# Flamingo-style gated block on one core: seven block products for eight at two more places, and one batch's layer-norm statistics on ScalarE

## The chip, the cores and the metric

The kernel runs on one core of a Trainium2 chip. The metric is device time in microseconds, the median of three runs. Names of the engines: PE is TensorE (matmul; PEld is its weight load), DVE VectorE, ACT ScalarE, POOL GpSimd, SP SyncE (which here only issues DMAs).

## The reference

```python
def fake_quant(x, scale, zp):              # scale 8/255, zp 128
    q = jnp.clip(jnp.round(x / s + z), 0.0, 255.0)
    return (q - z) * s
def xattn(x1, x2):                         # (2,1024,2048) by (2,2048,2048)
    return jnp.matmul(fake_quant(x1, ...), fake_quant(x2, ...))
def ffn(x, weight):                        # weight (2048,2048)
    s = 127.0 / jnp.clip(jnp.max(jnp.abs(x), axis=-1, keepdims=True), 1e-05, None)
    xq = jnp.clip(jnp.round(x * s), -128.0, 127.0) / s
    scale_w = 1.0 / jnp.clip(jnp.mean(jnp.abs(weight)), EPS, None)
    tw = jnp.clip(jnp.round(weight * scale_w), -1.0, 1.0)
    return jnp.einsum('bsi,oi->bso', xq, tw) / scale_w
...
x = x + jnp.tanh(g_xattn[0]) * xattn(_layernorm(x), ctx_4096)
x = x + jnp.tanh(g_ffn[0]) * ffn(_layernorm(x), weight)
```

x is (2, 1024, 2048), the context (2, 2048, 2048), one matrix for each batch; the ternary weights serve both batches.

## The kernel before, in words

**Tiles.** The 2 x 1024 rows are 16 tiles of 128, t = 0 to 7 for batch 1 and 8 to 15 for batch 2. A product of a row tile has 2048 columns, in halves h of 1024 and quarters q of 512. `resid` has eight rows of slots, so the x of tile t + 8 is loaded where tile t stood, once that one's output has been stored.

**First product.** `norm1` (L536) takes a pair of tiles: mean and variance on DVE (`bn_stats` L542, four to a tile; `bn_aggr` L547), a square root on ACT (L551), small DVE steps, and the quantised rows in int8 on ACT (L578). `turn_steps` (transposes on PE, L505, and casts to fp16 on ACT or DVE, L513) or `turn_far` (a transposing DMA, L478, and casts, L484) makes the transposed tile aT. `context` (L593) loads a 1 MB chunk of context, quantises it on ACT (L604) and clips it on DVE (L608). `first(t, h)` (L621) is 32 matmuls of 128 x 512 (L633) into one PSUM tile of two banks (`mm`, three of them), and one 1024-wide eviction into `resid` on DVE (L639), which also sums the row into a column of `acc`.

**Second product.** `norm2` takes the mean from `acc` (L665), squares on ACT (L671), the row maximum on DVE (L677) and quantises (L727). `qT` is the transposed result. Weights come as 1 MB rows (`weight_load`), are summed (L1001, L1003), scaled, cast (L1039), transposed on PE (L1046) and clipped to fp8 by ACT or DVE (L1054, L1056). Batch 1's tiles 0 to 3 go two by two through `couple` (L778, matmuls L770), which puts a quarter of two row tiles into the two halves of one `mm` tile and evicts each half (L754, 512 wide); tiles 4 to 7 through `plain` (L803, matmuls L816). Batch 2 goes through `seven` (L892, matmuls L941): two row tiles by two column halves by two halves of the contraction are eight block products, and by the scheme of Strassen and Winograd seven are enough, with sums of row blocks made on DVE (L906 to L913) and differences of weight blocks, T1 to T4. `differences` (L835) makes those on DVE (L853) and stores them to DRAM (L872); `bring_back` (L876) loads them when the SBUF is free; its "T3" is loaded over weights that are no longer used.

**Order.** Nothing is emitted at once. Every piece is a `step` of a planner (`Order`) with an engine (or a choice of DVE and ACT), a cost in us, a due time, what it reads and writes, and slots to take from a pool: "ar" (32 slots of the arena in SBUF), "q8" (five int8 rows), "mm" (three PSUM tiles), "tr" (two banks for transposes). The planner makes a list schedule, improves it over a list of random seeds (`shake`), and `give_out` emits every instruction in the planned order. On the chip each engine runs its queue strictly in that order; the waits between engines are put in by the framework from the data that instructions share.

There is a second path, `general`, for other zero points; it does not run.

## Time and profile before

| | |
|---|---|
| median of 3 runs | 475.76 us (475.75 to 476.7) |
| the profiled execution | 475.75 us, of which the span from first to last instruction is 473.9 us |
| granted TensorE clock | 0.999 |
| PE's first product starts | 18.47 us |
| the last of PE's waits over 0.4 us ends | 37.21 us |
| DMA | 105.33 MB, mean 222 GB/s |

The shares of busy time in 40 slices of the span, in tenths (9 is 90% or more):

```profile
PE   0499999999999999999999999999999999999994
DVE  4878977697896896669998985174673887743442
ACT  3986897786999998950356783001472745600000
PEclk9999999999999999999999999999999999999999
DMA  8999999993359758759999652039220125422133
```

PE is full from the second slice to the last but one. A slice is 11.8 us. DVE has full slices around 210 to 250 us, where the weight differences and the statistics of batch 2 lie, and few after; ACT is full from about 118 to 190 us, where the weights are quantised and transposed, and stands idle for much of 190 to 235 us and of the time after 300 us.

### The profile page before, as it was taken

To read this page: it belongs to the slowest core of one execution; us is meant where nothing else is said; L and a number is where in the kernel's file an instruction comes from. 1 tells how busy PE (TensorE), PEld (TensorE's weight loads), DVE (VectorE), ACT (ScalarE), POOL (GpSimd) and SP (SyncE) were. 2 spreads that over 40 slices of the span, in tenths; PEclk is the share of its full clock that TensorE was granted. 3 is DMA by queue.
4 is the path that set the end of the run, shared out by engine and by line. 5 is a ranking of instruction groups with operands and counts; after the bars stand their busy time and mean duration, and the time that the engine had idled before them with its cause. 6 is when DMAs were issued, how large, how long until landed. Compare 5 with 4: busy or idle time off the path is not lost.

```text
span 473.9 us, 6127 instructions
## 1 busy us (share of the span) xinstructions
PE 449.3 (95%) x2468; PEld 219.6 (46%) x2468; DVE 335.0 (71%) x528; ACT 263.9 (56%) x204; POOL 21.4 (5%) x39
## 2 busy tenths in 40 slices
PE   0499999999999999999999999999999999999994
PEld 0244444445577645444444444444444444444442
DVE  4878977697896896669998985174673887743442
ACT  3986897786999998950356783001472745600000
POOL 0000000000011111111111000000000000000000
PEclk9999999999999999999999999999999999999999
DMA  8999999993359758759999652039220125422133
GB/s 314 405 413 414 413 416 346 344 428 142 147 210 345 275 169 308 261 194 339 418 422 367 232 76 58 0 109 342 84 44 1 21 68 134 133 91 89 46 155 116
DMA packets 34528, 105.33 MB, mean 222 GB/s; under 512 B 14652, under 2 KB 14652, under 8 KB 29372
## 3 DMA queue, kind: packets, MB, share of 16 engines
q1 hardware_dynamic: 27680, 70.26, 40.1%
q0 software_dynamic: 6800, 34.61, 20.5%
q8 instruction: 21, 0.34, 0.3%
q14 instruction: 15, 0.12, 0.1%
q10 hardware_dynamic: 12, 0.00, 0.0%
HBM read 80.74 MB, written 20.97 MB: 215 GB/s over the span
## 4 chain that ended last, share of the span: by engine, by line
PE 82%; DMA 5%; DVE 5%; ACT 4%; issue 1%; SPq 0%; ACTq 0%
PE mm L633 41%; PE mm L941 20%; PE mm L816 11%; PE mm L770 8%; DMA resid<-in_x_dram 3%; DMA arena<-in_ctx_dram 2%; ACT bytes L1039 2%; PE tr L505 1%; DVE arena L1056 1%; DVE strip L677 1%; DVE arena L513 1%; PE tr L1046 1%; ACT arena L513 1%; DVE resid L754 1%; ACT arena L1054 1%
## 5 line engine op out<-in xcount | busy, mean ns | idle before, releaser
L633 PE MATMUL mm<-arena 128*128 128x512 f16 x1024 | 226.3, 380 | 3.9 <-DVE arena L608 3.9
L633 PEld LDWEIGHTS <-arena 128*128 128x128 f16 x1024 | 99.6, 98 | 120.9 <-issue 5.9
L941 PE MATMUL mm<-arena 128*128 128x512 fp8e4 x448 | 97.0, 379 | 0.0
L604 ACT ACTIVATE arena<-arena,scal 128x2048 int16<-128x2048 f32 x32 | 62.9, 1998 | 60.4 <-DMA arena<-in_ctx_dram 60.3
L754 DVE SCALAR_TENSOR_TENSOR resid<-mm,am,resid 128x1024 f32<-128x1024 f32 (+1 forms) x53 | 57.5, 1099 | 49.2 <-PE mm L941 36.2
L941 PEld LDWEIGHTS <-arena 128*128 128x128 f16 x448 | 43.9, 98 | 52.8
L639 DVE SCALAR_TENSOR_TENSOR resid<-mm,scal,resid 128x1024 f32<-128x1024 f32 x32 | 40.8, 1280 | 38.4 <-PE mm L633 36.4
L770 PE MATMUL mm<-arena 128*128 128x128 fp8e4 (+1 forms) x448 | 58.5, 288 | 0.1
L816 PE MATMUL mm<-arena 128*128 128x512 fp8e4 x256 | 56.4, 379 | 0.0
L671 ACT ACTIVATE arena<-resid,strip 128x2048 f32<-128x2048 f32 x16 | 32.0, 1998 | 27.3 <-DVE strip L665 14.2
L770 PEld LDWEIGHTS <-arena 128*128 128x128 f16 x448 | 33.5, 98 | 23.0 <-issue 0.3
L677 DVE TENSOR_REDUCE strip<-arena 128x1 f32<-128x2048 f32 x16 | 36.4, 2280 | 8.5 <-ACT arena L671 8.5
L542 DVE BATCH_NORM_STATS2 stats<-resid 128x6 f32<-128x512 f32 x64 | 40.0, 679 | 2.6 <-DMA resid<-in_x_dram 2.6
L853 DVE TENSOR_TENSOR arena<-arena 128x2048 fp8e4<-128x2048 fp8e4 x16 | 36.2, 2281 | 5.2 <-PE mm L633 5.2
L816 PEld LDWEIGHTS <-arena 128*128 128x128 f16 x256 | 24.8, 98 | 28.8
L727 ACT ACTIVATE bytes<-resid,strip 128x2048 int8<-128x2048 f32 x16 | 32.9, 2090 | 8.3 <-DVE strip L700 8.0
L578 ACT ACTIVATE bytes<-resid,strip 128x2048 int8<-128x2048 f32 (+1 forms) x17 | 33.0, 1985 | 5.9 <-DVE strip L561 5.9
L1039 ACT ACTIVATE bytes<-arena,scal 128x2048 int8<-128x2048 f32 x16 | 31.6, 2002 | 1.2 <-DVE scal L1025 1.2
L1056 DVE TENSOR_SCALAR arena<-tr 128x1024 fp8e4<-128x1024 int8 x22 | 26.2, 1217 | 4.9 <-ACT arena L1054 2.8
L513 ACT CAST arena<-tr 128x1024 f16<-128x1024 int8 x23 | 22.4, 1010 | 8.9 <-PE tr L505 8.6
L484 ACT CAST arena<-arena 128x1024 f16<-128x1024 int8 x21 | 21.6, 1041 | 7.0 <-DVE arena L484 3.8
L513 DVE CAST arena<-tr 128x1024 f16<-128x1024 int8 x17 | 20.3, 1219 | 3.2 <-PE tr L505 2.0
(63 smaller groups left out, 195.8 us busy)
## 6 DMA issues: line engine op xcount, KB each, us to landing
arena<-in_ctx_dram SPq DMA_DIRECT2D x16, 1024.0 KB, 14.0
arena<-in_L_ffn_weight_dram SPq DMA_DIRECT2D x16, 1024.0 KB, 7.6
arena<-in_ctx_dram POOLq DMA_DIRECT2D x16, 1024.0 KB, 7.5
out_dram<-resid SPq DMA_DIRECT2D x31, 512.0 KB, 3.1
arena<-in_L_ffn_weight_dram POOLq DMA_DIRECT2D x9, 1024.0 KB, 5.3
resid<-in_x_dram POOLq DMA_DIRECT2D x8, 1024.0 KB, 8.8
resid<-in_x_dram SPq DMA_DIRECT2D x7, 1024.0 KB, 17.7
awayT<-arena SPq DMA_DIRECT2D x8, 512.0 KB, 8.0
```

What stands on the lines that cost most here:

```text
L513: (nc.scalar.copy if engine == "ACT" else nc.vector.tensor_copy)(d[:, ts(h, n)], v[:, ts(h, n)])
L542: nc.vector.bn_stats(stats6[:, t % 4, c, :], res(t)[:, ts(c, 512)])
L604: nc.scalar.activation(slot16(slots[0]).bitcast(I16), s["w"], AF.Identity, scale=rs2)
L633: nc.tensor.matmul(pm[t][:, ts(q, U)], a[:, c, j, :], o[:, j, ts(q, U)], start=(c + j == 0), stop=(c + j == C),)
L639: nc.vector.scalar_tensor_tensor(v, pm[t], g1, v, ALU.mult, ALU.add, accum_out=acc[:, i : i + 1])
L677: nc.vector.tensor_reduce(s["vm"][:, n + i : n + i + 1], s["dev", t], AX.X, ALU.max)
L754: lambda: nc.vector.scalar_tensor_tensor(v, ps(), am2[:, t : t + 1], v, ALU.mult, ALU.add),
L770: nc.tensor.matmul(ps[:, o0 * P : o1 * P], a[:, c, j, :], w[:, j, o0:o1], start=(c + j == 0), stop=(c + j == C),)
L816: nc.tensor.matmul(s["pm"][:, ts(i, U)], a[:, c, j, :], w[:, j, :], start=(c + j == 0), stop=(c + j == C),)
L853: nc.vector.tensor_tensor(slot8(s[k, n])[:, w], slot8(at(a))[:, w], slot8(at(b))[:, w], op, saturate=False)
L941: nc.tensor.matmul(s[bank][:, ts(n, U)], a[:, c, j, :], v[:, c, j], start=new and c + j == 0, stop=c + j == 4, skip_group_check=not new,)
L1039: nc.scalar.activation(s["q"], wl[ot]["w"], AF.Identity, scale=sw)
```

## The change

- **`seven_first`, `context_sums`**: in batch 2's first product, columns 1024 to 2047 of tiles 10 to 15 are computed in pairs with seven products of eight matmuls each. The context's differences T1, T2 and T4 get six arena slots, T3 overwrites columns of four context units, and waits until tiles 8 and 9 have used these.
- **PSUM**: the pool "mm" has six halves for three tiles; `first`, `couple`, `plain` and `seven` take two halves (`both`), `seven_first` takes single halves. Each of its products is evicted 512 wide; `acc` gets a third column for these tiles, and `norm2` adds it.
- **Tiles 6 and 7** of batch 1 go through `seven` too, with the weight differences from SBUF (`near`). `differences` is therefore placed ahead of batch 1's last tiles (hold 150 instead of 210), and `bring_back` loads all four differences into new slots, under other gates.
- **x statistics of batch 2** (`on_act`): per tile two ACT passes with an accumulator, sum and then sum of squares about the mean.
- **Smaller**: weights ask for certain arena slots first (`w_slot`), `turn_far` leaves two slots free for qT, and `shake` draws with its own generator and another list of seeds, so the whole order is drawn anew. `two_steps` is empty.

```diff
@@ room, pools
-        if prefer is None:
+        if prefer is None and k == 2:
+            prefer = range(0, len(pool) - 1, 2)
+        elif prefer is None:
...
-    acc = const.tile([P, 2 * MT], F32, name="acc")
+    acc = const.tile([P, 3 * MT], F32, name="acc")
+    def both(slots):
+        return mm[slots[0] // 2]
-    plan = Order({"ar": NS, "q8": NB, "mm": 3, "tr": 2})
+    plan = Order({"ar": NS, "q8": NB, "mm": 6, "tr": 2})
+    on_act = set(range(MT, 2 * MT))
+    two_steps = set()
@@ norm1
+        def sum_of(i, t):
+            if "ac" not in s:
+                s["ac"] = tiny(2 * n)
+            nc.scalar.activation(junk, res(t), AF.Identity, accum_out=s["ac"][:, i : i + 1])
+        def shift():
+            s["nm"] = tiny(n)
+            nc.vector.tensor_scalar(s["nm"], s["ac"][:, 0:n], -1.0 / K, None, ALU.mult)
+        def square_of(i, t):
+            nc.scalar.activation(
+                junk, res(t), AF.Square, bias=s["nm"][:, i : i + 1], accum_out=s["ac"][:, n + i : n + i + 1]
+            )
...
+        if tiles[0] in on_act:
+            for i, t in enumerate(tiles):
+                step("ACT", 2.25, due, lambda i=i, t=t: sum_of(i, t), rd=xk(t), wr=[key("s1", i)])
+            step("DVE", 0.2, due, shift, rd=[key("s1", i) for i in range(n)], wr=[key("nm")])
+            for i, t in enumerate(tiles):
+                step("ACT", 2.25, due, lambda i=i, t=t: square_of(i, t), rd=xk(t) + [key("nm")], wr=[key("s2", i)])
...
@@ new functions after first
+    def context_sums(b, h, due, spent):
+        unit = lambda c, n: slot16(cx[b, h, c]["a"]).rearrange("p (j n) -> p j n", j=2)[:, :, ts(n, U)]
+        makers = {}
+        all_in = [cx[b, h, c]["by"] for c in range(C)] + [turned["aT", t, "by"] for t in range(b * MT, b * MT + MT)]
+        todo = (("T1", (0, 1), (0, 0)), ("T2", (1, 1), "T1"), ("T4", (1, 0), "T2"), ("T3", (1, 1), (0, 1)))
+        ones = []
+        for k, u, v in todo:
+            for c in range(4):
+                def at(v, c):
+                    if isinstance(v, tuple):
+                        return unit(4 * v[0] + c, v[1])
+                    return tx[v].rearrange("p (c j n) -> p c j n", c=4, j=2)[:, c]
+                def go(slots=None, k=k, u=u, v=v, c=c, at=at):
+                    if slots is not None:
+                        tx[k] = arena[:, slots[0] * SLOT : slots[0] * SLOT + 2 * SLOT]
+                    o = unit(c, 1) if k == "T3" else at(k, c)
+                    nc.vector.tensor_tensor(o, at(u, c), at(v, c), ALU.subtract)
+                rd, give = [], []
+                for w in (u, v):
+                    if isinstance(w, tuple):
+                        rd.append(("ca", b, h, 4 * w[0] + c))
+                        give.append(cx[b, h, 4 * w[0] + c]["by"])
+                    else:
+                        rd.append(("tx", w, c))
+                        give.append(makers[w])
+                m = step(
+                    "DVE", 0.42, due, go, rd=rd, wr=[("tx", k, c)], give=give,
+                    take=("ar", 2, 0, pairs_d) if c == 0 and k != "T3" else None,
+                    then=[spent[c], ones[c]] if k == "T3" else [makers[k]] if c else all_in,
+                )
+                if k == "T1":
+                    ones.append(m)
+                if c == 0:
+                    makers[k] = m
+        return makers
...
+    def seven_first(ta, tb, h, due, makers):
+        s = {}
+        b = ta // MT
+        by_seven.update((ta, tb))
+        W = 4 * 2 * P
+        def half(t, i):
+            return slot16(turned["aT", t])[:, ts(i, W)]
+        def sums(i, slots=None):
+            if slots is not None:
+                v = arena[:, slots[0] * SLOT : slots[0] * SLOT + 2 * SLOT]
+                s[1], s[2], s[4] = (v[:, ts(j, W)] for j in range(3))
+            if i == 0:
+                nc.vector.tensor_add(s[1], half(tb, 0), half(tb, 1))
+            elif i == 1:
+                nc.vector.tensor_tensor(half(tb, 0), half(ta, 0), half(tb, 0), ALU.subtract)
+                s[3] = half(tb, 0)
+            elif i == 2:
+                nc.vector.tensor_tensor(s[2], s[1], half(ta, 0), ALU.subtract)
+            else:
+                nc.vector.tensor_tensor(s[4], half(ta, 1), s[2], ALU.subtract)
+        qa, qb = ([("aT", t, i) for i in range(2)] for t in (ta, tb))
+        ga, gb = turned["aT", ta, "by"], turned["aT", tb, "by"]
+        by = step("DVE", 0.7, due - 3, lambda slots: sums(0, slots), rd=qb, wr=[("R", ta, 1)], take=("ar", 2, 0, pairs_d), give=[gb], then=[makers["T4"]])
+        step("DVE", 0.7, due - 3, lambda: sums(1), rd=qa[:1], wr=qb[:1] + [("R", ta, 3)], give=[ga, gb])
+        step("DVE", 0.7, due - 3, lambda: sums(2), rd=qa[:1] + [("R", ta, 1)], wr=[("R", ta, 2)], give=[ga, by])
+        step("DVE", 0.7, due - 3, lambda: sums(3), rd=qa[1:] + [("R", ta, 2)], wr=[("R", ta, 4)], give=[ga, by])
+        products = (
+            ("P1", "A", lambda: half(ta, 0), (0, 0), qa[:1], True, (ta, 0), ga),
+            ("P2", "C", lambda: half(ta, 1), (1, 0), qa[1:], True, (ta, 0), ga),
+            ("P6", "A", lambda: s[2], "T2", [("R", ta, 2)], False, (ta, 1), by),
+            ("P5", "B", lambda: s[1], "T1", [("R", ta, 1)], True, (tb, 1), by),
+            ("P7", "A", lambda: s[3], "T3", [("R", ta, 3)], False, (tb, 1), gb),
+            ("P3", "B", lambda: s[4], (1, 1), [("R", ta, 4)], False, (ta, 1), by),
+            ("P4", "A", lambda: half(tb, 1), "T4", qb[1:], False, (tb, 0), gb),
+        )
+        takes = {}
+        seen = set()
+        for k, (name, bank, left, right, need, new, dest, left_by) in enumerate(products):
+            def mult(cs, slots=None, bank=bank, left=left, right=right, new=new):
+                if slots is not None:
+                    s[bank] = mm[slots[0] // 2][:, ts(slots[0] % 2, U)]
+                a = left().rearrange("p (c j m) -> p c j m", c=4, j=2)
+                for c in cs:
+                    if isinstance(right, tuple):
+                        v = slot16(cx[b, h, 4 * right[0] + c]["a"]).rearrange("p (j n) -> p j n", j=2)[:, :, ts(right[1], U)]
+                    elif right == "T3":
+                        v = slot16(cx[b, h, c]["a"]).rearrange("p (j n) -> p j n", j=2)[:, :, ts(1, U)]
+                    else:
+                        v = tx[right].rearrange("p (c j n) -> p c j n", c=4, j=2)[:, c]
+                    for j in range(2):
+                        nc.tensor.matmul(
+                            s[bank], a[:, c, j, :], v[:, j, :],
+                            start=new and c + j == 0, stop=c + j == 4, skip_group_check=not new,
+                        )
+            for i, cs in enumerate(((0, 1), (2, 3))):
+                if isinstance(right, tuple):
+                    b_keys = [("ca", b, h, 4 * right[0] + c) for c in cs]
+                else:
+                    b_keys = [("tx", right, c) for c in cs]
+                give = [left_by]
+                if isinstance(right, tuple):
+                    give += [cx[b, h, 4 * right[0] + c]["by"] for c in cs]
+                elif right == "T3":
+                    give += [cx[b, h, c]["by"] for c in cs]
+                else:
+                    give.append(makers[right])
+                take = i == 0 and new
+                m = step(
+                    "PE", 0.855, due + 1.75 * k, (lambda f, cs: lambda slots=None: f(cs, slots))(mult, cs),
+                    rd=need + b_keys, wr=[("wc", ta, bank)], take=("mm", 1) if take else None, give=give,
+                )
+                if take:
+                    takes[bank] = m
+            t, n = dest
+            last = dest in seen or dest == (tb, 0)
+            col = 2 * (t % MT) + 1 if n == 0 else 2 * MT + t % MT
+            def add(t=t, n=n, bank=bank, last=last, col=col):
+                v = res(t)[:, h * H + n * U : h * H + (n + 1) * U]
+                kw = dict(accum_out=acc[:, col : col + 1]) if last else {}
+                nc.vector.scalar_tensor_tensor(v, s[bank], g1, v, ALU.mult, ALU.add, **kw)
+            step(
+                "DVE", 0.8, due + 1.75 * (k + 1), add, rd=[("wc", ta, bank), ("g1",)],
+                wr=xk(t, h) + ([("acc", col)] if last else []),
+                give=[takes[bank]],
+            )
+            seen.add(dest)
@@ norm2, mean
+            if t in by_seven:
+                u = 2 * MT + t % MT
+                nc.vector.scalar_tensor_tensor(
+                    m, acc[:, a : a + 1], acc[:, a + 1 : a + 2], acc[:, u : u + 1], ALU.add, ALU.add
+                )
+                nc.vector.tensor_scalar(m, m, -1.0 / N, None, ALU.mult)
@@ bring_back
-                    wt[k, n] = wt[2 + n, 0] if k == "T3" else slots[0]
+                    wt[k, n] = slots[0]
...
-                    take=None if k == "T3" else ("ar", 1, 0, home_w), dma=1.4,
+                    take=("ar", 1, 0, home_w), dma=1.4,
@@ seven
-                    b = wt[right[0], n] if isinstance(right[0], str) else wt[right[0] + n, right[1]]
+                    if isinstance(right[0], str):
+                        b = near[0][right[0], n] if near else wt[right[0], n]
+                    else:
+                        b = wt[right[0] + n, right[1]]
@@ the order of the parts
-    for t in range(4, MT):
+    near = differences(due, "SP", 150.0)
+    for t in (4, 5):
         for h in range(2):
             plain(t, h, due)
             due += 6.9
+    seven(6, 7, due, near=near)
+    due += 24.2
     s1 = due
...
-    for h in range(2):
-        for t in range(MT, 2 * MT):
-            first(t, h, due)
-            due += 6.9
+    for t in range(MT, 2 * MT):
+        first(t, 0, due)
+        due += 6.9
+    spent = []
+    for t in (MT, MT + 1):
+        spent = first(t, 1, due)
+        due += 6.9
+    makers = context_sums(1, 1, due - 12.0, spent)
+    for t in range(MT + 2, 2 * MT, 2):
+        seven_first(t, t + 1, 1, due, makers)
+        due += 12.0
...
-    differences(s1 - 40.0, "SP", 210.0)
-    bring_back(s1 + 60.0, "SP", [("acc", 2 * i) for i in range(MT)])
+    gate = {"T2": [("acc", 11)], "T1": [("R", 14, 4)], "T3": [("R", 14, 4)], "T4": [("R", 14, 4)]}
+    bring_back(s1 + 60.0, "SP", gate)
```

## The prediction

> **What bounds the kernel now.** I read the busy line first, then TensorE's waits, then the chain that ended last.
>
> ```profile
> PE 449.3 (95%) x2468; PEld 219.6 (46%) x2468; DVE 335.0 (71%) x528; ACT 263.9 (56%) x204; POOL 21.4 (5%) x39
> PE tr L436 <- ACT row L2008: 7.5, 1, 7.5
> PE tr L505 <- ACT bytes L578: 5.0, 2, 4.4
> PE mm L633 <- DVE arena L608: 3.9, 2, 3.4
> PE tr L505 <- ACT arena L513: 1.4, 1, 1.4
> 168.31 0.67 DVE resid L754
> 169.02 3.61 PE mm L770 x16
> 267.44 101.01 PE mm L633 x468
> 373.63 94.12 PE mm L941 x436
> 467.77 0.75 DVE resid L754
> ```
>
> The reader is to see that TensorE (PE) is the bound. Its waits sum to about 18 us, nearly all of it before 37 us, while the first rows and context arrive. From 40 us on the windows of 20 us show PE busy for 19.4 to 20.0 of each. The chain of waits leaves PE from 126 to 169 us, for DVE and ACT work that ends in a stall of only 0.1 to 0.3 us; from 169 us it is matmuls and transposes alone, and ends with one 512-wide eviction and its store. A 512-wide matmul costs 101.01 / 468 = 0.216 us in the chain (94.12 / 436 = 0.216); the "mean 380 ns" of the groups is a pipelined duration and is not used. So a matmul removed saves 0.216 us, unless PE then waits.
>
> **What is removed on PE.** A pair of row tiles by half the columns took 64 matmuls in `first` and takes 7 x 8 = 56 in `seven_first`: three pairs, 24 fewer. Tiles 6 and 7 took 4 x 32 = 128 in `plain` and take 112 in `seven`: 16 fewer. 40 x 0.216 = **-8.6 us**.
>
> **What moves between the other engines.** The prices come from these rows (busy sum, then mean ns of one):
>
> ```profile
> L542 DVE BATCH_NORM_STATS2 stats<-resid 128x6 f32<-128x512 f32 x64 | 40.0, 679 | 2.6 <-DMA resid<-in_x_dram 2.6
> L547 DVE BATCH_NORM_AGGREGATE strip<-stats 128x2 f32<-128x24 f32 x16 | 3.8, 251 | 0.3
> L1003 ACT ACTIVATE junk<-arena 128x2048 int8<-128x2048 f32 x8 | 15.2, 1902 | 3.1 <-DMA arena<-in_L_ffn_weight_dram 3.0
> L1003 ACT ACTIVATION_READ_ACCUMULATOR junk<-arena 128x1 f32 x8 | 1.5, 186 | 0.0
> L671 ACT ACTIVATION_READ_ACCUMULATOR arena<-resid,strip 128x1 f32 x16 | 3.0, 190 | 0.0
> L906 DVE TENSOR_TENSOR arena<-arena 128x1024 f16<-128x1024 f16 x4 | 2.7, 686 | 0.1
> L754 DVE SCALAR_TENSOR_TENSOR resid<-mm,am,resid 128x512 f32<-128x512 f32 x18 | 13.3, 746 | 11.7 <-PE mm L770 10.8 <-PE mm L941 0.9
> 200.00:220.00 20.00, 20.00 (x95) 9.02 (x93) 16.22 (x14) 8.01 (x5) 3.19 (x5) 1.00 0.70 241
> 220.00:240.00 20.00, 20.00 (x94) 9.07 (x93) 19.93 (x22) 4.31 (x3) 3.04 (x5) 1.00 1.01 413
> 240.00:260.00 20.00, 20.00 (x106) 9.59 (x105) 17.45 (x33) 12.67 (x9) 1.81 (x3) 1.00 1.02 390
> 260.00:280.00 20.00, 20.00 (x106) 9.50 (x105) 18.75 (x40) 14.70 (x12) 0.53 (x1) 1.00 0.53 176
> 280.00:300.00 20.00, 20.00 (x94) 9.11 (x93) 9.44 (x13) 8.32 (x8) 0.00 (x0) 1.00 0.28 53
> ```
>
> The windows give, after the length, the busy us of PE, weight load, VectorE (DVE), ScalarE (ACT) and GpSimd.
>
> DVE loses 32 x 0.679 + 8 x 0.251 = 23.7 us of batch 2's statistics. It gains 16 context sums (`context_sums`) and 12 row sums of 0.686, 19.2; 4 row sums for tiles 6 and 7, 2.7; 21 evictions of 0.746 in place of 6 of 1.280 (L639), 8.0; 7 evictions of 1.281 in place of 4 (L754, 1024 wide), 3.8; and six small ones of 0.2. Net about +11, of which 19.2 + 8.0 fall after 280 us, where the windows show DVE half idle. On the path: nothing as a sum; what counts is who waits at each hand-over, below.
>
> ACT gains 8 x (1.902 + 0.186) for the sums and 8 x (1.998 + 0.190) for the squares (L671's Square is 1998 ns): 34.2 us. The rows of 200 to 300 us hold 48.0 of 100, so they would hold 82.2. ACT's queue is in program order: behind each x pass stand context quantisations (L604) and casts of transposed rows (L513), and PE waits for these. Walking the changed order with these durations, the transposed rows of tile 9 are ready about 5 us before PE reaches them, and those of 14 and 15 over 10 us before. So the cost taken is 0; if the cover fails it is the second rival.
>
> The DMA steps keep their kinds and order on SP and GpSimd up to the weight loads. The weight differences (L853) are made earlier and still stored away; tiles 6 and 7 use them from SBUF. The bring-backs are gated later, and land about 5 us before their products. `bring_back`'s "T3" takes new slots, so it no longer waits for the weights it overwrote. Cost 0.
>
> **What the change adds: waits inside the PSUM tiles.** `seven_first` counts a two-bank tile of PSUM as two halves and gives different block products to the two halves of one tile. In the changed program the waits follow whole tiles: a product into one half waits for the eviction of the other, and an eviction waits for the latest matmul into either half. The trace has this case already: `couple` puts two row tiles into the halves of one tile, and the rows at 168.31 and 169.02 show the matmuls for the second half starting 0.04 us after the first half's eviction ended, though the transposes before them were done at 168.88.
>
> The price of one such wait, if nothing stands between: the last matmul of 373.63 + 94.12 starts near 467.37 and its eviction at 467.77, 0.40 later; the eviction takes 0.75, PE follows 0.04 later, and 0.216 is the matmul's own slot: 0.40 + 0.75 + 0.04 - 0.216 = 1.0 us. The pairs (10,11), (12,13), (14,15) are interleaved, and the changed order has four of them bare: P2 of the second pair behind P5 of the first; half of P3 of the first behind P2 of the second; half of P7 of the second behind P4 of the first; half of P3 of the third behind its own P2. Three more are covered by four to eight matmuls (0.86 to 1.73 us) except for 0.1 to 0.2. 4 x 1.0 + 3 x 0.13 = **+4.4 us**. Bounds: 0 if the halves are independent on the chip; 7 x 1.0 = 7 if the covered ones are not covered.
>
> The Trainium skill, "PSUM — Partial Sum Buffer", section "Summary: rules for kernel authors", says that reading PSUM while a matmul runs is done by targeting a different bank, with semaphores by bank. The halves here are different banks, so by the page no wait would be needed, and the sum would be 4.4 us lower; the rows at 168.31 and 169.02 show that this program waits all the same, and I go by them.
>
> **The redrawn order.** The planner's random draws change, so the whole order does. In the head, the first weight clip shifts PE's first product from 18.47 to about 19.5, and tile 5's transposes stand behind a context quantisation whose data lands at 51; walked through, PE is 0.4 us further behind its work at 100 us: **+0.4**, bounds 0 and 1.5. From 100 to 200 us the order before loses 1.4 us (PE's start minus its summed work grows from 21.45 at 108 to 22.86 at 193). In the changed one two half-tile waits in `couple` are bare (0.95 and 0.45) and the rest roughly covered: 1.4 again, so **0**, bounds -1.4 and +2. The end is the same as before: four matmul pieces, a 512-wide eviction, a 256 KB store.
>
> Sum on the profiled execution: 473.9 - 8.6 + 4.4 + 0.4 = 470.1 us of span. The execution took 475.75, 1.86 more than its span, and the median is 475.76, so the forecast is **472.0 us**, 0.8% faster. About 0.2% (1 us) is what a measurement of this kernel can tell from no change.
>
> **Rivals.** *The halves cost nothing*: the evictions stay off PE's path. For it: DVE is half idle after 280 us. Against: the rows at 168.31. 472.0 - 4.4 = 467.6. 20%.
>
> *No change, by VectorE ahead of the pairs*: the planner counts 0.42 us for a context sum, L906 says 0.686; 16 x 0.266 = 4.3 us of lateness just ahead of `seven_first`, with its row sums and evictions queued behind. P5's row sum is ready only about 1 us early, so 3.3 could reach PE: 475.3. Against: DVE's idle share there can absorb it. 9%.
>
> *Slower, by ScalarE at the batch boundary*: ACT was idle 52.0 of 200 to 300 us, but 26.2 of that ended with context landing (15.5, 4.7, 2.9, 2.8, 0.2 of its L604 groups), which the x passes can't freely fill if they stand behind a late load; DMA is at 1.01 and 1.02 in two windows. Then 25.8 is left for 34.2, ACT ends 8.4 late, and PE waits for tile 9's or a later tile's rows: up to 472.0 + 8.4 = 480.4, with half of the 5 us margin kept 477.9. It decides against the change from 4.7 us of PE waits between 240 and 330 us. For it: the load there more than doubles. Against: the passes need only x, which can be resident early. 16%.
>
> **How the numbers follow.** 55% for the forecast, its own range 470 to 474.5. Faster: 55 + 20 = 75%; same 9%; slower 16%. The range: below, the first rival with a better middle part, 467.6 - 0.8 = 466.8; above, 477.0, which takes in the no-change case and the milder part of the slow one, and leaves out some 11%.
>
> **What would show it.** Matmul count down by 40, with 0.216 us each in the chain. In the PE waits, the changed eviction of `seven_first` as releaser, about 4 us in all, with PE gaps of about 1 us right after 512-wide evictions near 330 to 360 us: if they are missing, the first rival holds. PE waits for x bytes or cast rows between 240 and 330: the slow rival. PE waits for row sums or context sums: the no-change rival. A different start of PE's gapless run than about 37.6 us would make the +0.4 wrong. The prediction is wrong as a whole if PE is not gapless from 100 us on apart from these.

## The result and the profile after

The changed kernel takes 477.11 us (median of 10 runs, 476.37 to 478.01), the kernel before 475.63 (10 runs, 475.18 to 476.7). The ratio is 1.0029, with a 95% interval of 1.0018 to 1.0040: slower by 0.3%, where 0.8% faster was forecast. The profiled execution has a span of 475.0 us against 473.9.

The page of the changed kernel:

```profile
span 475.0 us, 6130 instructions
...
PE 442.3 (93%) x2428; PEld 216.1 (45%) x2428; DVE 344.2 (72%) x554; ACT 296.3 (62%) x237; POOL 21.6 (5%) x39
```

PE has 40 matmuls fewer, as the change says, and does 7 us less of busy time; yet the span grew. DVE has 9 us more and ACT 32. TensorE's waits (total, times, longest):

```profile
PE tr L450 <- ACT row L2244: 7.5, 1, 7.5
PE mm L704 <- DVE arena L660: 6.3, 1, 6.3
PE tr L519 <- ACT bytes L630: 5.2, 2, 4.6
PE mm L829 <- DVE resid L860: 3.4, 4, 0.8
PE mm L1036 <- DVE resid L974: 1.8, 1, 1.8
PE mm L990 <- DVE resid L974: 1.5, 2, 0.8
PE tr L1271 <- DVE arena L1281: 1.0, 1, 1.0
```

The first three were there before. The wait ahead of the first product, for the first clipped context, grew from 3.4 to 6.3, and 7.7 us of waits are new, all for DVE: for evictions of `seven_first` (L860), for evictions of batch 1's second product (L974), and for a weight clip (L1281).

To place them I use one number from the traces, *PE's lateness*: the start of a matmul less the work that PE has done before it, at 0.2158 us for 512 columns and 0.0557 for 128. (16 matmuls of 128 columns take 0.89 us in the chains of both kernels.) It grows where PE stands, waits that the list of waits does not name included, and where its matmuls run slower than at these prices, as they do in the head (see `head` below). In us, by the work done:

| PE's lateness at this much work | before | after | grew more by |
|---|---|---|---|
| 100 us | 21.30 | 23.05 | 1.75 |
| 140 us | 22.25 | 24.11 | 0.1 |
| 190 us | 22.67 | 27.99 | 3.5 |
| 300 us | 22.69 | 28.24 | 0.2 |
| the end | 22.71 | 32.57 | 4.3 |

Less work, 8.63, and more lateness, 9.86, make +1.2; the spans differ by 1.1.

The new waits in the timeline of the changed kernel (start, us, engine and line; in brackets the idle time ahead and who ended it):

```profile
177.91 2.28 DVE L1073 TENSOR_TENSOR arena<-arena 128x2048 fp8e4<-128x2048 fp8e4 x1
...
180.11 2.35 DVE L1281 TENSOR_SCALAR arena<-tr 128x1024 fp8e4<-128x1024 int8 x2
...
182.51 0.61 PE L1271 MATMUL tr<-ident,bytes 128*128 128x128 f16 x8 [0.96 <-DVE arena L1281]
...
195.07 2.28 DVE L1073 TENSOR_TENSOR arena<-arena 128x2048 fp8e4<-128x2048 fp8e4 x1
...
199.28 0.74 DVE L974 SCALAR_TENSOR_TENSOR resid<-mm,am,resid 128x512 f32<-128x512 f32 x1
...
200.07 1.89 PE L1036 MATMUL mm<-arena 128*128 128x512 fp8e4 x8 [1.80 <-DVE resid L974]
```

At 177.91 a weight difference (L1073, 2.28 us) starts on DVE; two weight clips stand behind it, and PE's transposes wait for them until 182.51. At 195.07 another one stands ahead of a `norm2` chain and an eviction, and PE's matmuls wait until 200.07 for a PSUM tile. How full DVE is there, in two windows of the changed kernel (us; then PE, weight load, DVE, ACT and GpSimd busy, the granted clock, the DMA share and GB/s):

```profile
180.00:200.00 20.00, 17.31 (x104) 8.64 (x102) 16.56 (x26) 15.07 (x12) 1.41 (x2) 1.00 0.65 209
200.00:220.00 20.00, 19.31 (x101) 9.21 (x101) 18.91 (x15) 12.84 (x9) 1.23 (x2) 1.00 0.68 231
```

DVE is not full in either, and PE waits for it all the same.

In `seven_first` the chain of waits shows what the prediction had (start, us, what):

```profile
335.15 3.47 PE mm L829 x16
338.61 0.03 issue
338.64 0.76 DVE resid L860
339.40 0.04 issue
339.44 2.76 PE mm L829 x12
```

The last matmul of a product starts near 338.2; the eviction from the one half takes from 338.64 to 339.40; 0.04 later PE goes on in the other half. Lateness grows by 1.01 us here and three more times, at 343.04, 358.00 and 368.66.

The groups of the work that was moved or added (count, busy us, mean ns, idle before):

```profile
L1073 DVE TENSOR_TENSOR arena<-arena 128x2048 fp8e4<-128x2048 fp8e4 x16 | 36.2, 2282 | 0.5 <-PE mm L1036 0.4
...
L587 ACT ACTIVATE junk<-resid,strip 128x2048 int8<-128x2048 f32 x8 | 16.0, 1996 | 0.7 <-DVE strip L584 0.6
...
L580 ACT ACTIVATE junk<-resid 128x2048 int8<-128x2048 f32 x8 | 15.2, 1902 | 13.5 <-DMA resid<-in_x_dram 13.4
...
L860 DVE SCALAR_TENSOR_TENSOR resid<-mm,scal,resid 128x512 f32<-128x512 f32 x21 | 15.3, 748 | 8.1 <-PE mm L829 8.0
...
L752 DVE TENSOR_TENSOR arena<-arena 128x1024 f16<-128x1024 f16 x16 | 10.4, 686 | 0.5 <-PE mm L704 0.4
```

Every duration is that of the prediction within 0.01 us. The ACT passes wait 13.4 us for x; the slow rival had feared waits for context and had called x resident early. But lateness grows by only 0.25 us from 190 to 300 us of work, where these passes lie: PE waited little for ACT.

### The profile page after: what moved, and what is told of

Its sections match the earlier page's. It is cut to its first block, busy times and chain, and to the rows that moved or that the text cites. A ratio compares the mean times of both kernels' runs of the same rounds, so it can differ in the third digit from the quotient of the medians.

```text
span 475.0 us, 6130 instructions
## 1 busy us (share of the span) xinstructions
PE 442.3 (93%) x2428; PEld 216.1 (45%) x2428; DVE 344.2 (72%) x554; ACT 296.3 (62%) x237; POOL 21.6 (5%) x39
## 4 chain that ended last, share of the span: by engine, by line
PE 85%; DVE 6%; DMA 5%; ACT 2%; issue 1%; ACTq 0%
PE mm L704 35%; PE mm L1164 24%; PE mm L990 10%; PE mm L829 8%; PE mm L1036 5%; DMA arena<-in_ctx_dram 4%; DVE arena L1073 2%; PE tr L519 2%; PE tr L1271 1%; DVE resid L974 1%; DMA row<-in_g_ffn_dram 1%; DVE arena L1281 1%; DVE resid L860 1%; DVE stats L556 1%; ACT bytes L630 1%
## 5 line engine op out<-in xcount | busy, mean ns | idle before, releaser
L704 PE MATMUL mm<-arena 128*128 128x512 f16 x832 | 185.6, 382 | 6.4 <-DVE arena L660 6.3
L704 PEld LDWEIGHTS <-arena 128*128 128x128 f16 x832 | 81.1, 99 | 102.0 <-issue 7.2
L1164 PE MATMUL mm<-arena 128*128 128x512 fp8e4 x560 | 122.0, 379 | 0.0
L974 DVE SCALAR_TENSOR_TENSOR resid<-mm,am,resid 128x1024 f32<-128x1024 f32 (+1 forms) x56 | 61.9, 1109 | 46.8 <-PE mm L1164 35.7
L1164 PEld LDWEIGHTS <-arena 128*128 128x128 f16 x560 | 54.7, 98 | 65.7 <-issue 0.3
L990 PE MATMUL mm<-arena 128*128 128x128 fp8e4 (+1 forms) x448 | 58.3, 288 | 1.5 <-DVE resid L974 1.5
L710 DVE SCALAR_TENSOR_TENSOR resid<-mm,scal,resid 128x1024 f32<-128x1024 f32 x26 | 33.2, 1279 | 18.1 <-PE mm L704 18.1
L990 PEld LDWEIGHTS <-arena 128*128 128x128 f16 x448 | 33.3, 98 | 23.4 <-issue 1.7
L829 PE MATMUL mm<-arena 128*128 128x512 f16 x168 | 37.9, 379 | 3.4 <-DVE resid L860 3.4
L1073 DVE TENSOR_TENSOR arena<-arena 128x2048 fp8e4<-128x2048 fp8e4 x16 | 36.2, 2282 | 0.5 <-PE mm L1036 0.4
L498 ACT CAST arena<-arena 128x1024 f16<-128x1024 int8 x20 | 20.6, 1042 | 15.5 <-DVE arena L498 8.2
L1036 PE MATMUL mm<-arena 128*128 128x512 fp8e4 x128 | 28.4, 379 | 1.8 <-DVE resid L974 1.8
L829 PEld LDWEIGHTS <-arena 128*128 128x128 f16 x168 | 16.4, 97 | 24.1 <-issue 4.8
L660 DVE TENSOR_SCALAR arena<-arena 128x2048 f16<-128x2048 int16 x32 | 21.4, 685 | 5.8 <-ACT arena L656 5.8
L1281 DVE TENSOR_SCALAR arena<-tr 128x1024 fp8e4<-128x1024 int8 x20 | 23.7, 1217 | 2.4 <-PE tr L1271 1.7
L527 DVE CAST arena<-tr 128x1024 f16<-128x1024 int8 x19 | 22.8, 1217 | 3.3 <-PE tr L519 2.5
```

The costliest lines, as they stand in the source:

```text
L704: nc.tensor.matmul(pm[t][:, ts(q, U)], a[:, c, j, :], o[:, j, ts(q, U)], start=(c + j == 0), stop=(c + j == C),)
L710: nc.vector.scalar_tensor_tensor(v, pm[t], g1, v, ALU.mult, ALU.add, accum_out=acc[:, i : i + 1])
L829: nc.tensor.matmul(s[bank], a[:, c, j, :], v[:, j, :], start=new and c + j == 0, stop=c + j == 4, skip_group_check=not new,)
L974: lambda: nc.vector.scalar_tensor_tensor(v, ps(), am2[:, t : t + 1], v, ALU.mult, ALU.add),
L990: nc.tensor.matmul(ps[:, o0 * P : o1 * P], a[:, c, j, :], w[:, j, o0:o1], start=(c + j == 0), stop=(c + j == C),)
L1036: nc.tensor.matmul(s["pm"][:, ts(i, U)], a[:, c, j, :], w[:, j, :], start=(c + j == 0), stop=(c + j == C),)
```

## The experiments

All but the four named as drawn anew keep the changed kernel's planned order, apart from the edit shown; numbers in the edits are steps of the plan. `order` is the list in which steps are given out, `slots` the buffers, `where` the engine. Line numbers shift by some lines with an edit.

### late_diff: three differences a few places back

```diff
+ for n, at, m in ((537, 1, 451), (538, 1, 515), (539, 1, 538), (532, 1, 518)):  # 537, 538, 532: differences; 539: a store
+     order.remove(n)
+     order.insert(order.index(m) + at, n)
```

> The changed kernel in its own order, but three weight differences (L1073) stand behind the work they stood ahead of on VectorE: one behind two weight clips, one behind an eviction, one behind another eviction. Nothing is added or left out. Theory A (the weight differences, moved ahead of batch 1's last tiles, delay evictions and clips that PE waits for): the waits of PE that ended at 182.51, 200.07 and 206.93 us in the changed kernel (1.1, 2.0 and 0.8 us) shrink to 0, 0 and about 0.5; span 475.0 - 3.4 = 471.6. Rival B (VectorE and ScalarE are simply full there, and another wait takes the place): less than 1 us is gained, span above 474.0.

Measured: span 474.9, median 476.92. The waits that ended at 182.51 and 200.07 are gone, but the work that the differences now stand ahead of is late in its turn. The timeline of this kernel:

```profile
184.77 1.21 DVE L1284 TENSOR_SCALAR arena<-tr 128x1024 fp8e4<-128x1024 int8 x1
...
186.08 1.02 ACT L1282 ACTIVATE arena<-tr 128x1024 fp8e4<-128x1024 int8 x1 [3.46 <-DVE arena L1284]
...
187.15 0.61 PE L1274 MATMUL tr<-ident,bytes 128*128 128x128 f16 x8 [0.94 <-ACT arena L1282]
...
198.03 2.28 DVE L1076 TENSOR_TENSOR arena<-arena 128x2048 fp8e4<-128x2048 fp8e4 x1
...
201.37 0.74 DVE L977 SCALAR_TENSOR_TENSOR resid<-mm,am,resid 128x512 f32<-128x512 f32 x1
...
202.16 3.61 PE L993 MATMUL mm<-arena 128*128 128x512 fp8e4 x16 [1.42 <-DVE resid L977]
```

The clip at 184.77 stands behind two evictions, so ACT's clip comes at 186.08 and PE's transposes at 187.15. The difference at 198.03 is now ahead of the next eviction, which PE awaits until 202.16. Lateness still grows by 3.3 us between 140 and 190 us of work, where the changed kernel has 3.9. So 0.6 us was gained, and the time is as rival B had it. Theory A, that a few differences stand in the wrong place, fell for these three moves: they only shifted the waits.

### no_diff: the differences left out

```diff
- s[k, n] = slots[0]
...
- nc.vector.tensor_tensor(slot8(s[k, n])[:, w], ..., op, saturate=False)
+ s[k, n] = wt[n, 0]
```

> The changed kernel in its own order without the 16 weight differences (L1073) on VectorE; the products and stores take a block of weights in their place, so all other work stays. Left out: 36.2 us of VectorE. Moving three of them back by a few places only moved the waits. Theory B (VectorE is full from 150 to 260 us since the differences stand there): PE's lateness, which in the changed kernel grows by 3.9 us while it does the work from 140 to 190 us, grows by less than 1.0; span near 475.0 - 3.3 = 471.7 or lower. Rival (ScalarE's weight quantisation or the order of PE's queue sets these waits): it still grows by 3 us or more.

Measured: span 471.7 in one execution. Lateness grows from 23.42 to 24.01 between 140 and 190 us of work, 0.6 instead of 3.9. Its waits behind the head:

```profile
PE mm L829 <- DVE resid L860: 3.4, 4, 0.9
PE mm L990 <- DVE resid L974: 1.2, 2, 0.8
PE mm L704 <- ACT arena L527: 0.5, 1, 0.5
```

No wait for a weight clip, none for `plain`'s tile; what is left for L990 is the two waits inside `couple`. Without the differences 3.3 of the 3.9 us are gone, while ScalarE's work was the same (296.5 us busy against 296.3). This is one execution, and it shows that the differences are the cause, not yet whether by their amount or by their place.

### halves: the same products in other halves

```diff
+ for n, k in ((874, (2,)), (858, (5,)), (883, (1,)), (908, (5,)), (902, (1,)), ...):
+     slots[n] = list(k)
+ order.remove(876); order.insert(order.index(847), 876)   # one eviction ahead of two row sums
```

> The changed kernel in its own order, with the block products of seven_first put into other halves of the same three PSUM tiles, so that no product follows at once on an eviction in the other half of its tile; one eviction stands two row sums earlier on VectorE. Theory A (waits follow whole tiles): the four waits of 1.01 us at 339.4, 343.0, 358.0 and 368.7 us vanish; span 475.0 - 4.0 = 471.0. Rival (PE waits there for VectorE's evictions as such, or the chip cannot read one bank and write its neighbour): the waits stay, span above 474.0.

Measured: span 471.9, median 473.30, ratio to the kernel before 0.9951 (0.9934 to 0.9967). The waits of `seven_first` (here L834 for L865) shrank from 3.4 to 0.2, while those of batch 1 stayed:

```profile
PE mm L1041 <- DVE resid L979: 1.8, 1, 1.8
PE mm L995 <- DVE resid L979: 1.5, 2, 0.8
PE tr L1276 <- DVE arena L1286: 1.0, 1, 1.0
PE mm L709 <- DVE arena L532: 0.6, 1, 0.6
PE mm L834 <- DVE resid L865: 0.2, 1, 0.2
```

Lateness over the three pairs grows by 0.55 instead of 4.3. So the waits were those of the halves, and a choice of halves in which no product follows on an eviction of its neighbour removes them without less work. The span is 3.1 us shorter; 0.8 more than in the changed kernel is lost at the batch boundary, most of it in the wait of 0.6 for a cast on DVE.

### couple_evict: the same order on every engine, one wait turned around

```diff
+ order.remove(494); order.insert(order.index(493) + 1, 494)   # eviction of tile 2 behind tile 3's last piece
```

> The changed kernel with one eviction of couple (L974, tile 2) given out behind the last matmul piece of tile 3, whose half lies in the same PSUM tile, instead of ahead of it. The order on each engine is the same as before; only which of the two waits for the other is turned around. Theory A (waits follow whole PSUM tiles in the order in which instructions are given out): the wait of 0.84 us that ends at 157.54 vanishes and PE is 1.0 us earlier from there on; what remains of it at the end depends on VectorE: between 0 and 1.0, span 474.0 to 475.0. Rival (the second half waits for VectorE for some other reason): the wait at 157.54 stays.

Measured: span 473.7, median 476.44. Lateness at 140 us is 22.71, where the kernels with the same head and the old order have 23.4 to 24.4: the wait at 157 us is gone, and its 1.0 us stays gone to the end of this execution. By the medians the gain cannot be told from none (ratio to the kernel before 1.0025, 1.0011 to 1.0039; the changed kernel has 1.0029). No queue was changed. The order in which an eviction from one half and the products into the other are given out decides which of them waits: here the eviction starts at 157.17, behind the last matmul into the other half, where in the changed kernel the matmuls waited for it until 157.54. So the wait follows the whole tile, and the program sets it. Whether the chip could write one half while the other is read was not run.

### head: the first context chunk first

```diff
+ for n, at, m in ((45, 0, 48), (46, 0, 49), (47, 0, 34)):   # load, quantisation, clip
+     order.remove(n); order.insert(order.index(m) + at, n)
+ slots[45], slots[48] = [24, 25], [26, 27]
```

> The changed kernel in its own order but for the head: the first context chunk is loaded, quantised and clipped ahead of the second, as in the kernel before, and its clip stands ahead of three statistics on VectorE. Theory A (the redrawn head costs what PE's lateness at 100 us shows, 23.05 against 21.30 us): PE's first product starts near 18.5 us instead of 20.79, lateness at 100 us falls by 0.7 to 1.5; span 473.6 to 474.3. Rival (the lateness there comes from transfers that land late): the first product starts earlier, but lateness at 100 us stays within 0.3 of 23.05, span 474.7 to 475.3.

Measured: span 474.1, median 476.46; PE's first product starts at 18.66, lateness at 100 us is 21.64. That looked like theory A. But at 50 us of work, where this run has 21.61, the same edit in two later versions has 22.69 (`three`) and 23.06 (`five_head`) with the same early start, and without the edit six executions have 22.1 to 23.0. PE's waits in these three heads agree within 0.1 us, so they are not the difference. The pace of the matmuls is. The twelve matmuls from 22.4 us on, here (L709) and in `five_head` (L711):

```profile
22.49 3.73 PE L709 MATMUL mm<-arena 128*128 128x512 f16 x12
22.42 5.25 PE L711 MATMUL mm<-arena 128*128 128x512 f16 x12
```

The same twelve take 3.73 us in one execution and 5.25 in the other, 1.5 us more, and the lateness differs by 1.45. At 0.2158 us each they would start within 2.6 us. (The column of the granted clock reads 1.00 for these windows in both; the pace has to be read from the rows.) So the head of one program differs by 0.9 to 1.5 us between executions, here by how long its first matmuls run slowly, and a gain of 1 us from the edit was not confirmed. What ends the slow stretch is not shown here.

### three: the edits that worked alone, together

> The changed kernel in its own order with the three edits that worked alone: the other halves in seven_first, the eviction of couple behind the second half's matmuls, the head's first context chunk. The gains alone were 3.4, 1.0 and 1.0 us of PE's lateness. If they add up: lateness at the end 32.6 - 0.4 (what the first look of the changed kernel had more than its later ones) - 5.4 = 26.8, span 469.3, 1% below the kernel before. Rival (PE, earlier by 2 us, only runs into VectorE again between 150 and 210 us, where it is full): the waits there grow by 1 to 2 us, span 470.5 to 471.5.

Measured: span 471.3, median 472.79, ratio 0.9949 (0.9932 to 0.9965). The edits of `halves` and `couple_evict` add up. The head's gain does not show: lateness is 22.69 at 50 us of work, by the slower matmuls above, and a wait of 0.8 us for the end of the weight sum at 115 us of the timeline adds 1.0. Between 140 and 190 us of work lateness still grows by 3.9, so the span is where the rival put it, but not by the rival's longer waits.

### five: the queue of DVE rearranged for what PE waits for

```diff
+ for n in (455, 471):                       # two weight clips to ScalarE
+     where[n] = "ACT"
+ for n, at, m in ((876, 0, 847), (494, 1, 493), (537, 1, 451), (515, 1, 514), (538, 1, 511), (539, 1, 538), (518, 1, 394), (519, 1, 518)):
+     order.remove(n)                        # 515, 518: evictions
+     order.insert(order.index(m) + at, n)
```

The edit of the halves is in it too, that of the head is not.

> The changed kernel in its own order with the other halves in seven_first, the eviction of couple behind the second half's matmuls, and VectorE's queue from 178 to 210 us rearranged: evictions and casts that PE waits for stand ahead of four weight differences, and two weight clips go to ScalarE (2.4 us less on VectorE). Theory B (VectorE's queue there is too full for the differences, and what counts is what stands behind them): the growth of PE's lateness while it does the work from 140 to 190 us falls from 3.9 to 1.5 or less; span 475.0 - 3.4 - 1.0 - 2.4 = 468.2 or lower. Rival (the waits only move on, as with the first rearrangement): growth 3 or more, span 470 or more.

Measured: span 465.8, median 468.37, ratio to the kernel before 0.9857 (0.9841 to 0.9874). Its waits of PE, those for the first row, context and bytes left out, one window as above, and two rows of its DVE:

```profile
PE mm L711 <- DVE arena L534: 0.5, 2, 0.3
PE mm L836 <- DVE resid L867: 0.2, 1, 0.2
```

```profile
200.00:220.00 20.00, 20.00 (x100) 9.31 (x99) 20.00 (x14) 10.45 (x8) 1.80 (x3) 1.00 0.67 240
```

```profile
195.33 0.75 DVE L981 SCALAR_TENSOR_TENSOR resid<-mm,am,resid 128x512 f32<-128x512 f32 x1 [0.48 <-PE mm L997]
196.00 6.68 DVE L1080 TENSOR_TENSOR arena<-arena 128x2048 fp8e4<-128x2048 fp8e4 x3
```

All 16 differences are done, but the three at 196.00 now stand behind the eviction at 195.33, where in the changed kernel one stood ahead of the `norm2` chain and the eviction. DVE is busy for 20.00 of the 20 us from 200 to 220, more than the 18.91 of the changed kernel, and PE waits for none of it: lateness grows by 0.1 between 140 and 190 us of work. In this kernel a full DVE is no bound as long as what stands at the head of its queue is what PE needs next. Two things were changed at once, the order and two clips of 1.2 us moved to ScalarE, and no run parts them. Its median is the lowest of all runs, though the intervals of `five_head` and `costs2` overlap with its own, and 1.4% below the kernel before.

### five_head

> The fastest version so far (the changed kernel's order with the other halves, the eviction of couple and VectorE's queue from 178 to 210 us rearranged) with the head's first context chunk first, too. If the head's 1.0 us is real, PE's lateness at 100 us is 1.0 less than the 22.1 there, span 464.8; if it only shifts the wait (as in the version with three edits, where lateness at 100 us was 23.7), span 465.5 to 467.5.

Measured: span 466.3, median 469.06, ratio 0.9869 (0.9852 to 0.9885); lateness at 100 us 23.10, against 22.13 without the edit. The head's edit brings nothing that can be shown, since the pace of the first matmuls differs by more.

### Four orders drawn anew

*plain67*: tiles 6 and 7 back in `plain`, `differences` back at `s1 - 40.0`, 10 new seeds.

> The changed kernel with tiles 6 and 7 of batch 1 back in plain and the weight differences back where the kernel before has them; the rest of the change stays. The order is drawn anew with 10 seeds of its own. 16 matmuls more on PE, 3.45 us. Theory B (the seven products for tiles 6 and 7 bring 36 us of weight differences into a full VectorE): the lateness between 100 and 210 us grows by at most 2.0 instead of 4.9; span 474.5 to 476.0, so the seven products there bring nothing. Rival (the waits there come from something else in the redrawn order): span 478 or more.

Measured: span 485.6, median 487.53, ratio 1.0259 (1.0242 to 1.0276). Theory B's expectation missed; the time is on the rival's side. Its head is 2.6 us later than the changed kernel's, and from 190 to 300 us of work it loses 5.4 us. The largest loss there is the mechanism again, although the differences were to come as late as in the kernel before: two of them, 4.49 us from 218.60, stand ahead of an eviction at 223.00, for which PE waits 2.45 us until 223.80. The run says nothing of the seven products; it says that an order drawn anew, here from 10 seeds where the changed kernel had 129, moves the time by more than the part that was to be measured.

*x_dve*: `on_act = set()`, 7 new seeds.

> The changed kernel with batch 2's x statistics back on VectorE (bn_stats); the rest of the change stays. The order is drawn anew with 7 seeds of its own. Theory B (VectorE is full from 150 to 280 us, so the 23.7 us that the statistics would put there must show): PE's lateness over that stretch grows by 2 us or more beyond the changed kernel's; span 477 or more. Rival (the statistics are hidden either way): span 474.0 to 475.5.

Measured: span 477.2, median 479.11, ratio 1.0067 (1.0047 to 1.0088). The time is as theory B had it, but 4.2 us of it is one place, in the timeline:

```profile
223.12 4.48 DVE L1073 TENSOR_TENSOR arena<-arena 128x2048 fp8e4<-128x2048 fp8e4 x2
...
227.51 1.94 DVE L974 SCALAR_TENSOR_TENSOR resid<-mm,am,resid 128x512 f32<-128x512 f32 x2
...
228.31 8.05 PE L1036 MATMUL mm<-arena 128*128 128x512 fp8e4 x29 [2.45 <-DVE resid L974]
```

Two differences, 4.48 us, stand ahead of the eviction at 227.51. That is the mechanism once more, yet no statistics stand on DVE from 195 us up to that eviction, so what the passes on ScalarE are worth stays open.

*costs2*: prices and tiles in the planner put right, 22 new seeds.

```diff
- w = 16 * (0.0255 + 0.0472 * (o1 - o0))
+ w = 16 * (0.0557 if o1 - o0 == 1 else 0.2158)
-     "DVE", 0.42, due, go, ...        # context sum
+     "DVE", 0.67, due, go, ...
- s[bank] = mm[slots[0] // 2][:, ts(slots[0] % 2, U)]   # and ("mm", 1)
+ s[bank] = both(slots)[:, 0:U]                         # and ("mm", 2)
- evict2(t, ..., due, [("cp", ta, q, i)], [by])
+ evict2(t, ..., due, [("cp", ta, q, 0), ("cp", ta, q, 1)], [by])
```

> The changed kernel with the planner's prices set to what the traces show: 0.0557 us for a matmul of 128 columns in couple instead of 0.0727 (256 of them, 4.4 us), 0.216 for one of 512, 0.67 for a context sum instead of 0.42; seven_first takes whole PSUM tiles, and both evictions of couple wait for both halves. The order is drawn anew with 22 seeds. Theory C (the plan of the changed kernel had PE 4.4 us too late in batch 1's second product, so it placed VectorE's work for a PE that comes later): with right prices the waits that the chip shows are those that the plan knows (1.6, 0.3 and 0.3 us after 100 us), lateness grows by 3 or less after 100 us; span 466 to 469. Rival (a redrawn order loses several us in places that no plan knows, as the two others drawn anew did): span 474 or more.

Measured: span 467.1, median 469.13, ratio 0.9870 (0.9852 to 0.9888). Lateness grows by 1.5 after 100 us, and over the pairs not at all: with whole tiles, `seven_first` has no waits. Prices, tiles and order changed at once, so the run does not tell what the prices alone bring.

*old_price*: the same with the 128-column matmul near its old price, 4 new seeds.

> As the kernel with corrected prices (whole PSUM tiles in seven_first, evictions of couple behind both halves), but with the price of a 128-column matmul in couple at 0.0740 us, near the old 0.0727, instead of 0.0557; a context sum 0.66. The order is drawn anew with the seeds that a search of the same length found (4). Theory C (the wrong price is what puts VectorE's work too late for PE): after batch 1's first couples PE runs 4.7 us ahead of its plan, and its lateness grows by 2.5 us or more while it does the work from 130 to 220 us; span 469.5 or more. Rival (whole tiles and the evictions of couple are enough, the price does not matter): growth below 1.5 there, span 468.5 or less.

Measured: span 469.0, median 470.64, ratio 0.9893 (0.9864 to 0.9922). Lateness grows by 2.0 between 130 and 220 us of work, between the two expectations, and one of its waits (0.4 us) is for a load of x. The right prices may be worth some 2 us, or the two searches only ended differently, and the intervals of the two ratios overlap; theory C stays open.

## Why the prediction was wrong

**Removed on PE**: right, 40 matmuls, 8.63 us.

**Waits inside the PSUM tiles**: right in mechanism and size. Forecast +4.4, measured +4.3, with the four bare waits at 1.01 us each. `halves` and `couple_evict` show that they come from the order and the choice of tiles, and `costs2` has none of them. The Trainium skill, "PSUM — Partial Sum Buffer", section "Summary: rules for kernel authors", has a reader use another bank than the running matmul, with semaphores by bank. The measurement decides against taking that for this program: its waits were there, four of 1.01 us.

**"The weight differences (L853) are made earlier ... Cost 0"**: this is the step that failed. They are 36.2 us of DVE work, moved in front of the evictions and clips by which batch 1's second product lives, and the growth of lateness from 100 to 210 us was +3.6 over the kernel before where the sum had 0. I asked where their data go and when, but not what stands behind them in DVE's queue; the DVE work I placed in time was only that after 280 us. DVE's busy time from 180 to 220 us rose from 13.95 and 16.22 of 20 us to 16.56 and 18.91. `no_diff` shows that the differences are the cause, with 3.3 us, and `five` that the price was avoidable.

**The head**: forecast +0.4, with PE's first product near 19.5; measured +1.75 in the profiled execution, with the first product at 20.79. Other executions of the same head give +0.8 to +1.3 over the one execution of the kernel before, so the term was too small in all of them; how much too small depends on how long the first matmuls ran slowly, which the sum had no term for.

**The waits of couple** in "the redrawn order": forecast 0.95 and 0.45, measured 1.01 and 0.78, the second lengthened by differences ahead of its eviction (in `no_diff` it is 0.56). "The rest roughly covered" was wrong, for the same reason as above.

**ACT at the batch boundary**: the cost of 0 nearly stood, 0.2 measured. That rival had the sign right, but the wrong engine and the wrong place, so a slower result is no point for it: the loss came from DVE, at 180 to 207 us of the timeline instead of 240 to 330.

The forecast of 470.1 for the span misses by 4.9: 3.6 between 100 and 210 us of work, nearly all of it from the differences, 1.35 in the head and 0.2 at the boundary, less 0.2 in small terms. The full saving of the first rival, 467.6, was nearly there to be had: `five` takes 468.37 with all of the change in it.

## What to carry to other kernels

When work is moved in time, price it at its new place: read the queue of its engine there, instruction by instruction, and ask which eviction or cast behind it another engine is waiting for; that the engine is not full there is no answer. When two products share a PSUM tile, look at the waits that the program really carries: alternate tiles, not halves, or give out the eviction behind the neighbour's matmuls. An order that a search has drawn is part of the kernel: to value one part, keep the order and edit it. The four orders drawn anew here took from 469.1 to 487.5 us, and `plain67`, 10 us above the changed kernel, had only 3.45 us more work on PE.

## What was not expected of the hardware

In `x_dve` a wait of 2.45 us cost 4.2 us of lateness, 2.6 of it reached by the first matmul behind the wait. The windows of 2 us there (the number ahead of the last two is the granted clock):

```profile
226.00:228.00 2.00, 0.00 (x0) 0.00 (x0) 2.00 (x2) 1.18 (x1) 0.00 (x0) 1.00 1.03 383
228.00:230.00 2.00, 1.69 (x5) 0.58 (x5) 2.00 (x3) 0.82 (x1) 0.00 (x0) 0.56 0.98 404
230.00:232.00 2.00, 2.00 (x7) 0.78 (x6) 2.00 (x2) 0.00 (x0) 0.65 (x2) 0.59 1.04 424
232.00:234.00 2.00, 2.00 (x11) 0.88 (x9) 2.00 (x4) 0.00 (x0) 0.59 (x1) 1.00 0.91 266
```

After the wait the clock was at 0.56 and 0.59 of full speed in two windows, then full again. By lateness the slower clock cost 1.6 us beyond the wait; `plain67` shows the same behind its wait of 2.45 us, 2.6 and 1.6 more. Waits of 1.8 us in the changed kernel left the clock at 1.00. So in these runs a wait of 2.45 us has a second price that one of 1.8 us had not; two cases do not fix where the step lies.

The Trainium skill, "TensorE: Matmul & The Clock Gate", section "What's actually happening", says that the clock falls to half after an idle window of about 3.4 us. Here a wait of 2.45 us was enough, so the measurement asks for a tighter limit than the page.
